# A four-layer transformer kernel on Trainium2: another order at the start of layer 0, at its seam with layer 1 and in layer 2, gates and experts' lists with the roles of their operands swapped, and experts every third slot

## The chip, the cores and the metric

The kernel runs on one core of one Trainium2 chip. TensorE (PE) multiplies matrices: it loads one operand, which stays (the stationary one, `lhsT`), and streams the other (the moving one, `rhs`) past it; results land in PSUM. VectorE (DVE), ScalarE (ACT) and GpSimd (POOL) do the rest, and SyncE (SP) issues most transfers. Every engine works through its own queue strictly in the order in which the kernel was written, and waits for others through semaphores. The metric is the device time of one execution in microseconds; lower is better.

## The reference

Four layers follow each other. Each is `x = x + attention(xn) + ffn(xn)` with `xn = layernorm(x)` over rows of 128; there are 4096 tokens in all.

- Layer 0, attention: an importance per token, relu(xn wi1) wi2, picks 76 tokens of each sequence of 256; 16 heads of 8 attend from all tokens to those. FFN: softmax gates over 8 experts; **each expert takes the 512 tokens with its highest gates** (of all 4096), computes `w2(silu(w1 x) * w3 x)`, and its rows are added back to their tokens.
- Layer 1, attention: 16 heads of 64 under a sparse causal mask. FFN: a sigmoid gate for each of 8 experts, the best two of each token, `down(relu(up(x w))**2)`.
- Layer 2, attention: 4 heads of 32 with learned windows. FFN: gated, then two hidden layers of 512 with gelu, then back to 128.
- Layer 3, attention: 16 heads of 64, causal. FFN: one quantized matrix and a low-rank one.

```python
x = x + L0_attn(xn) + L0_ffn(xn); xn = layernorm(x)
x = x + L1_attn(xn) + L1_ffn(xn); xn = layernorm(x)
x = x + L2_attn(xn) + L2_ffn(xn); xn = layernorm(x)
x = x + L3_attn(xn) + L3_ffn(xn)
```

All values are 32-bit floats, but for some masks and lists of integers in bf16, which holds them exactly.

## The kernel before, in words

**Tiling.** Tokens go in 8 chunks `c` of 512 (two sequences of 256; four tiles of 128 tokens with the token on the partition). `xnT` is a chunk turned, with the feature on the partition. PSUM has two double banks `sc`, two banks `tp`, one `mm` and one `po`. The order on all engines is written out by hand; no scheduler moves anything.

**Layer 0.** `begin` loads and normalizes chunks 0 to 3 and does the first chunk's preparation (`prelude`). Then `run` goes through slots `kk` from -8 to 69, eight to a chunk. In each slot it issues, for the chunk `c = kk // 8`, one `exps` (four scores of 32 rows and an exp over 1024 columns), for the next chunk one `maxima` (four more scores and their maxima on VectorE), and now and then `outputs`, `divided`, `turned` and `project`, which ends in `r[c]`, the chunk's attention. Beside them lanes advance by one step a slot. A lane is a generator; one step reaches to its next `yield`:

- `prelude(c + 2)`: importance (`ph`, `pi`), its column (`pcol`), ranks on VectorE, picks on GpSimd, queries (`queries0`), picked rows (`px`), keys (`pk`, then `ka` on GpSimd). `maxima` needs `ka`.
- `choice()`, from slot -3: 15 rounds find each expert's threshold bit by bit. A round compares on VectorE (`ge`), counts on TensorE and reduces on VectorE. Then come prefix sums and `vals`, the numbers of tokens as bf16.
- `expert(e)`, from slot `19 + 4 * e`: 0-1 comparisons with the places (`ohs`, four of 128 x 1024); the list `pix`, 32 matmuls that sum numbers under comparisons; ids; four gathers on GpSimd (`xr`); two slots on, the product with the gate on VectorE; transposes; up (four matmuls of 512 columns); down; and, nine slots after the start, four additions into `acc_d` in HBM by GpSimd's transfers.

`stats` and `root` are the two parts of a norm on VectorE, `apply` scales and shifts (three quarters on ScalarE, one on GpSimd), `turn` transposes and copies on ScalarE, `logits(c)` makes four matmuls with the turned chunk stationary and the 8 columns of `wg` moving, `gates` makes the softmax. `warm(n)` issues `n` matmuls of ones into an unused part of `po`; nothing reads their result. I call these fills. There are 122 of them. They sit in `begin` (62), at 6 a slot in slots -8, -7, -6 and -3 to 3.

**The seam.** When the experts have added their rows, `fetch(c)` reads a chunk of `acc_d` back on SP's queue (from slot 59 on; it waits for the last expert's additions) and `finish(c)` adds it to `r[c]` on GpSimd. Layer 1's norms, `Route.norms`, are lanes that start at slots 62 to 69; what is left of them goes on in layer 1's first steps. For each chunk they make stats, root, apply (all on ScalarE), transposes, and gates with the turned chunk stationary and 8 columns moving, followed by an exp.

**Layer 1** is a pipeline over 128 pairs of heads; `u` counts its steps from -5. A pair is projected, scored (first at `u = -3`), divided, turned and multiplied with its values. `Route.places`, the choice of two experts per token, goes beside it, one step a `u`, and must be done when `scatter` starts at `u = 14`.

**Layer 2** runs an iteration per chunk `f` with the attention of the next chunk `a` interleaved. `weights(f, 3)` transposes the last exps and copies them on VectorE (`p_eT`), `values(f, 1)` multiplies them (L1644), `back(f, 1)` turns and divides. They are issued like this:

```python
do(self.gated, f, 0); do(self.weights, f, 3)
do(self.gated, f, 1); do(self.values, f, 1); do(self.project, a, 0)
do(self.gated, f, 2); do(self.back, f, 1);   do(self.project, a, 1)
do(self.gated, f, 3);                        do(self.project, a, 2)
```

**Lines of the profile.** L354 fills; L406 turns of layer 0; L417 its logits; L456 and L461 a round's comparison and count; L546 and L558 an expert's comparisons and its list; L570 gathers; L577 product with the gate; L592 and L602 up and down; L616 additions to HBM; L736 maxima; L770 exps; L786 outputs; L1203, L1209, L1213, L1217 and L1221 the norms and gates at the seam (apply, transposes, copy, gates, exp). In rows of TensorE a 32-bit matmul counts as two (`x8` is four matmuls), a bf16 one as one.

## Time and profile before

| | |
|---|---|
| median of 3 runs | 2096.87 us (2095.76 to 2101.85) |
| the profiled execution | 2104.49 us, its span 2102.8 us |
| mean granted TensorE clock | 0.969 |
| TensorE busy | 2040.5 us, 97% |
| VectorE, ScalarE, GpSimd busy | 1217.0, 1081.9, 926.9 us |
| fills (L354) | 122, between 1.1 and 88.3 us |
| first maxima of slot -8 | 30.01 us |
| slot 0, slot 63 | 69.84, 377.21 us |
| layer 1's first scores | 425.5 us |
| layer 2, layer 3 from | 1086, about 1534 us |

The profile is of one execution. Busy time of TensorE is the time in which a matmul was under way, whatever its clock; the granted clock, given beside it as a share of full speed, says how fast it ran. In a list of rows in order of time, a bracket at a row's end tells how long the engine stood idle before it and who released it.

### The profile page before, as it was taken

How to read it: one execution, taken by the hardware profiler on the slowest of the kernel's cores; microseconds unless marked ns; L12 is line 12 of the kernel's file. 1: busy time of each engine (PE TensorE's matmuls, PEld its weight loads, DVE VectorE, ACT ScalarE, POOL GpSimd, SP SyncE). 2: the span in 40 equal slices, each digit the busy share in tenths (PEclk: the TensorE clock that was granted, in tenths of full speed). 3: DMA queues.
4: the chain of work that ended last, by engine and by line, in shares of the span. 5: the costliest groups of instructions: out<-in, count | busy, mean ns of one | idle time of the engine just before them, and what ended most of it. 6: DMA issues, size and time to landing. Idle time of an engine off the chain costs nothing.

```text
span 2102.8 us, 39083 instructions
## 1 busy us (share of the span) xinstructions
PE 2040.5 (97%) x13660; PEld 1392.1 (66%) x13660; DVE 1217.0 (58%) x4836; ACT 1081.9 (51%) x3166; POOL 926.9 (44%) x1360
## 2 busy tenths in 40 slices
PE   9999999799999999999999999999999999999998
PEld 6666666567777777776664555555477777777776
DVE  6777663586555544467774444443366566656654
ACT  3234454466665555565543444333376656566563
POOL 4005554336886555467661222233143444344433
PEclk7899999699999999999999999999999999999999
DMA  7500111400003444300010000000000000000000
GB/s 229 133 1 14 25 27 19 110 1 19 31 32 101 119 119 119 88 20 28 26 54 1 1 1 1 0 1 1 1 1 6 2 6 6 2 6 6 7 1 11
DMA packets 83208, 72.27 MB, mean 34 GB/s; under 512 B 14466, under 2 KB 74020, under 8 KB 82852
## 3 DMA queue, kind: packets, MB, share of 16 engines
q1 hardware_dynamic: 66352, 37.88, 6.3%
q0 software_dynamic: 15488, 31.61, 5.7%
q8 instruction: 108, 1.77, 0.3%
q14 instruction: 88, 0.72, 0.1%
q10 hardware_dynamic: 1172, 0.30, 0.1%
HBM read 49.70 MB, written 24.25 MB: 35 GB/s over the span
## 4 chain that ended last, share of the span: by engine, by line
PE 84%; DVE 9%; ACT 4%; issue 2%; POOL 1%; DMA 0%; DVEq 0%; POOLq 0%; ACTq 0%; SPq 0%
PE sc L1025 11%; PE sc L1688 10%; PE sc L1053 9%; PE po L1105 9%; PE tp L1091 8%; PE mm L1123 6%; PE sc L1038 5%; PE sc L770 2%; PE mm L1368 2%; PE tp L786 2%; PE sc L736 1%; ACT e L1070 1%; PE mm L1726 1%; PE sc L1601 1%; DVE e L1066 1%
## 5 line engine op out<-in xcount | busy, mean ns | idle before, releaser
L1081 POOL TENSOR_TENSOR e<-e,rs 128x256 f32<-128x256 f32 (+2 forms) x512 | 392.7, 788 | 528.2 <-DVE rs L1079 421.1
L1070 ACT ACTIVATE e<-e,mn 128x128 f32<-128x128 f32 (+2 forms) x1024 | 442.8, 434 | 124.6 <-DVE mn L1066 110.6
L1066 DVE CUSTOM_DVE_ANT_0 e<-sc,causal 128x128 f32<-128x128 f32 (+1 forms) x512 | 152.5, 354 | 175.3 <-PE sc L1053 175.3
L1092 DVE COPY eT<-tp 128x384 f32<-128x384 f32 x512 | 253.7, 537 | 0.1
L1066 DVE CUSTOM_DVE_ANT_0 e<-sc,sparse 128x128 f32<-128x128 f32 (+1 forms) x512 | 139.5, 328 | 162.7 <-PE sc L1053 147.2
L1688 PE MATMUL sc<-ff,h 128*128 128x512 f32 x512 | 229.8, 595 | 0.9 <-ACT ff L1703 0.5
L1091 PE MATMUL tp<-ident,e 128*128 128x128 f32 x1536 | 223.6, 282 | 0.0
L1091 PEld LDWEIGHTS tp<-ident,e 128*128 128x128 f32 x1536 | 163.6, 141 | 74.2 <-issue 54.0
L1070 ACT ACTIVATION_READ_ACCUMULATOR e<-e,mn 128x1 f32 x1024 | 191.4, 187 | 0.0
L1688 PEld LDWEIGHTS sc<-ff,h 128*128 128x128 f32 x512 | 93.4, 190 | 105.9 <-issue 101.2
L1123 PE MATMUL mm<-out,oT 128*128 128x128 f32 x1024 | 131.7, 283 | 7.8 <-ACT hb L1374 4.2
L1667 POOL TENSOR_TENSOR x<-l_o,x 128x256 f32<-128x256 f32 x16 | 11.9, 743 | 276.8 <-DVE l_o L1661 276.3
L1123 PEld LDWEIGHTS mm<-out,oT 128*128 128x128 f32 x1024 | 123.0, 197 | 14.9 <-ACT hb L1374 6.4
L1025 PE MATMUL sc<-m,qkv 128*128 128x256 f32 x512 | 126.1, 389 | 1.1 <-ACT m L1043 0.5
L1030 ACT ACTIVATE n<-sc 128x1024 f32<-128x1024 f32 x64 | 65.5, 1024 | 108.9 <-PE sc L1025 108.9
L1053 PE MATMUL sc<-n 64*128 64x128 f32 (+1 forms) x1024 | 118.5, 350 | 0.0
L1567 POOL TENSOR_SCALAR n<-dist,reach 128x256 f32<-128x256 f32 (+1 forms) x112 | 104.0, 929 | 18.8 <-DVE l_mn L1615 8.7
L1105 PE MATMUL po<-eT,p_v 128*64 128x256 f32 (+1 forms) x1024 | 111.5, 339 | 0.1
L1105 PE MATMUL po<-eT,m 128*64 128x256 f32 (+1 forms) x1024 | 111.4, 338 | 0.1
L1053 PE MATMUL sc<-qk 64*128 64x128 f32 (+1 forms) x1024 | 108.8, 331 | 1.4 <-DVE mn L1066 1.4
L1025 PEld LDWEIGHTS sc<-m,qkv 128*128 128x128 f32 x512 | 92.2, 190 | 20.3 <-ACT e L1070 7.9
L1030 ACT ACTIVATE qk<-sc 128x1024 f32<-128x1024 f32 x64 | 65.4, 1022 | 76.5 <-PE sc L1025 63.6
(399 smaller groups left out, 3827.5 us busy)
## 6 DMA issues: line engine op xcount, KB each, us to landing
xb<-zero SPq DMA_DIRECT2D x1, 4608.0 KB
xb<-xb SPq DMA_DIRECT2D x36, 128.0 KB
yb<-yb SPq DMA_DIRECT2D x36, 128.0 KB
x<-in_L_attn_x SPq DMA_DIRECT2D x8, 256.0 KB
m<-in_L_ffn_w SPq DMA_DIRECT2D x8, 256.0 KB
xn_d<-x SPq DMA_DIRECT2D x8, 256.0 KB
xa<-acc_d SPq DMA_DIRECT2D x8, 256.0 KB
h<-in_L_ffn_h_wT SPq DMA_DIRECT2D x2, 1024.0 KB
```

Source lines behind the costliest of these rows:

```text
L1025: nc.tensor.matmul(p[:, n, i * S : (i + 1) * S], lhsT=self.wqk[n][:, (2 * gg + i) * P : (2 * gg + i + 1) * P], rhs=(self.xk if n else self ...
L1030: self.pending.append(lambda: nc.scalar.activation(t.rearrange("p n i s -> p n (i s)"), p, AF.Copy))
L1038: nc.tensor.matmul(p[:, 0, t * S : (t + 1) * S], lhsT=self.xk[c][:, t0 : t0 + P], rhs=self.wv[:, gg * 256 : (gg + 1) * 256], start=True, s ...
L1053: nc.tensor.matmul(ps[:, j, c0:c1], lhsT=qk[r, 0, i, qt * P : (qt + 1) * P], rhs=qk[r, 1, i, k0 : k0 + c1 - c0], start=True, stop=True,)
L1066: nc.vector.tensor_tensor_reduce(out=e[:, j, c0:c1], in0=ps[:, j, c0:c1], in1=self.mask[:, c0:c1], scale=1.0, scalar=3e38, op0=ALU.add, op ...
L1070: nc.scalar.activation(e[:, j, c0:c1], e[:, j, c0:c1], AF.Exp, bias=m1, scale=-1.0, accum_out=sums[:, 2 * qt + j : 2 * qt + j + 1],)
L1081: nc.gpsimd.tensor_tensor(e[:, :, c0:c1], e[:, :, c0:c1], bcast(rs[:, 2 * qt : 2 * qt + 2], 2, c1 - c0), ALU.mult)
L1091: nc.tensor.transpose(pt[:, n * P : (n + 1) * P], e[:, j, c0 : c0 + P], k.ident)
L1092: nc.vector.tensor_copy(eT[:, j, :], pt[:, :384])
L1105: nc.tensor.matmul(o[64 * j : 64 * j + 64, t * P :], lhsT=v[:, t ^ self.swap, h : h + 64], rhs=eT[:, j, t * S : t * P + S], start=(t == 0) ...
L1123: nc.tensor.matmul(p[:, :D], lhsT=self.oT[s][:, n, t * P : (t + 1) * P], rhs=wo[:, n, :], start=(first is None and n == 0), stop=(n == 7),)
L1688: self.nc.tensor.matmul(ph, lhsT=self.w[wh][:, c, m * P : (m + 1) * P], rhs=src[c], start=(c == 0), stop=(c == NF - 1))
```

## The change

It has seven parts.

1. **Beginning.** Loads of `wg`, `wv` and `bv` go from ScalarE's queue to SP's. The norm of chunk 1 is by itself, and those of chunks 2 to 7 are one group of six; each apply, turn and logits step is dealt out to slots -8 to -4 with fills between. GpSimd's constants are made in three parts (`consts1` to `consts3`), two of them at slots -5 and -4. `prelude` issues the first query a slot earlier and `px` and `pk` on separate slots.
2. **Logits and layer 1's gates.** The gate matrix, padded to 32 columns, is stationary and four chunks' `xnT` of 512 columns each move, in four column groups of the array side by side. Four transposes bring the result back to tokens on partitions.
3. **Experts' lists.** The 8 columns of numbers are stationary and 128 columns of comparisons move; fourths of the tokens go to four column groups, after one matmul that zeroes the bank. ScalarE copies the four partial sums, and a slot later one matmul with `eighths` adds them up and turns them. The gathers stay in the same slot as before.
4. **Experts start every third slot**, at `19 + 3 * e`.
5. **The seam.** `fetch` goes out at slots 51 and 52 into tiles of its own, `finish` from slot 54. Layer 1's norms of chunks 0 to 6 are steps at fixed slots from 55 to 65 (`Route.early`, a quarter of the apply on GpSimd), gates of chunks 0 to 3 at 62 and 63. Chunk 7 and the other gates (`Route.last`) go before `places` in layer 1's first five steps.
6. **Fills**: 354 in all. 94 in `begin`; 5 a slot in -8 to 3, 2 in 12 to 18, 3 in 53 to 63, 5 from 64 on; 12 before the count of the choice's first two rounds and 4 before the others; 27 in the dealt-out steps; 4 in each of layer 1's first five steps.
7. **Layer 2.** `values(f, 1)` and `back(f, 1)` each move behind the next gated step.

```diff
 def logits(self, first):
-        for i in range(TT * c, TT * c + TT):
-            matmul(self.pg[:, i * NE : (i + 1) * NE], lhsT=self.xnT[c][:, i % TT * P : (i % TT + 1) * P], rhs=self.wg)
+        pl = self.bank()
+        for g in range(4):
+            nc.tensor.matmul(
+                pl[32 * g : 32 * g + 32, :], lhsT=self.wg, rhs=self.xnT[first + g], start=True, stop=True,
+                tile_position=(0, 32 * g),
+            )
+        rows = self.p2.tile([P, 2, CAP], F32, tag="g", name="lg", bufs=1)[:, 0, :]
+        nc.scalar.activation(rows, pl, AF.Copy)
+        yield
+        pt = self.bank()
+        for t in range(TT):
+            nc.tensor.transpose(pt[:, t * P : (t + 1) * P], rows[:, t * P : (t + 1) * P], k.ident)
+        nc.vector.tensor_copy(...)
 def choice(self):
+            self.warm(12 if i < 2 else 4)
 def expert(self, e):
         pix = k.po()
+        nc.tensor.matmul(pix[:, :P], lhsT=k.zero.bitcast(BF16)[:, :P], rhs=k.ones_b, start=True, stop=False)
         for t in range(32):
+            g = t % 4
             nc.tensor.matmul(
-                pix[:, :8], lhsT=ohs[t // 8][:, t % 8, :], rhs=self.vals[:, e, t, :, :].rearrange("p q v -> p (q v)"),
-                start=(t == 0), stop=(t == 31),
-            )
-        ixv = pix[:, :8].rearrange("p (q v) -> p q v", v=2)
+                pix[32 * g : 32 * g + 8, :P], lhsT=self.vals[:, e, t, :, :].rearrange("p q v -> p (q v)"),
+                rhs=ohs[t // 8][:, t % 8, :], start=False, stop=(t >= 28), tile_position=(0, 32 * g),
+            )
+        fourths = p2.tile([P, P], F32, tag="ohq", name="fourths")
+        nc.scalar.activation(fourths, pix[:, :P], AF.Copy)
+        yield
+        nc.tensor.matmul(pix[:, P : P + 8], lhsT=fourths, rhs=self.eighths, start=True, stop=True)
+        ixv = pix[:, P : P + 8].rearrange("p (q v) -> p q v", v=2)
...
         nc.vector.scalar_tensor_tensor(ids, ixv[:, :, 0], 128.0, two, ALU.mult, ALU.add)
-        yield
 def begin(self):
...
+            -8: [(self.stats, 6, 2, 6), (self.stats, 7, 2, 6), (self.root, 2, 6), (self.apply, 2), (self.apply, 3), warm],
+            -7: [
+                (self.turn, 2), warm, (self.apply, 4), (self.turn, 3), warm, (self.apply, 5), (next, a), warm,
+            ],
+            -6: [(self.turn, 4), (self.apply, 6), warm, (self.turn, 5), (next, a, 0), warm, (self.apply, 7), warm],
+            -5: [(self.turn, 6), warm, (self.turn, 7), warm, (next, b), (self.consts2,)],
+            -4: [(next, b, 0), (self.consts3,), (list, self.gates())],
 def run(self, tail):
-            starts[19 + 4 * e] = [self.expert(e)]
-        warm = {-8: 6, -7: 6, -6: 6, -3: 6, -2: 6, -1: 6, 0: 6, 1: 6, 2: 6, 3: 6}
-        loads = 19 + 4 * NE + 8
+            starts[19 + 3 * e] = [self.expert(e)]
+        warm = {kk: 5 for kk in range(-8, 4)} | {kk: 2 for kk in range(12, 19)} | {kk: 3 for kk in range(53, 64)}
+        loads = 19 + 3 * NE + 8
...
-                if kk == max(loads + c, 8 * c + 12) + 1:
-                    self.finish(c, xas.pop(c))
-                if kk == max(loads + c, 8 * c + 12):
-                    xas[c] = self.fetch(c)
+                if kk == loads + c // 4:
+                    xas[c] = self.fetch(c)
+                if kk == max(loads + 3 + c, 8 * c + 13):
+                    self.finish(c, xas.pop(c))
+            tail(kk)
+            if kk >= 64:
+                self.warm(5)
 class Route:
+    def early(self):
+        at = {}
+        for first, n in ((0, 2), (2, 2), (4, 2), (6, 1)):
+            for c in range(first, first + n):
+                u = 55 + c + c // 6
+                at.setdefault(u, []).append((self.stat, c, first, n))
+                for late, step in ((0, self.apply), (1, self.turn)):
+                    at.setdefault(57 + c + late, []).append((step, c))
+        at[62].append((self.gates, 0))
+        at[63].append((self.others, 0))
...
+    def last(self):
+        c = NC - 1
+        self.stat(c, c, 1); yield
+        self.root(c, 1); self.apply(c); yield
+        self.turn(c); yield
+        self.gates(c - 3); yield
+        self.others(c - 3)
 def layer1(...):
-    first = route.places()
+    first = chain(route.last(), route.places())
     def extra(u):
+        if u < 0:
+            warm(4)
 class Layer2:
             do(self.gated, f, 1)
-            if n:
-                do(self.values, f, 1)
             do(self.project, a, 0)
             do(self.gated, f, 2)
             if n:
-                do(self.back, f, 1)
+                do(self.values, f, 1)
             do(self.project, a, 1)
             do(self.gated, f, 3)
+            if n:
+                do(self.back, f, 1)
             do(self.project, a, 2)
```

`stat`, `root`, `apply`, `turn`, `gates` and `others` of `Route` do for layer 1 what `stats`, `root`, `apply`, `turn` and the two halves of `logits` do for layer 0; its `gates` puts the exp on the copy.

## The prediction

> **What bounds the kernel now.** I read the page's busy shares and slices first, then the busy time by stage, then TensorE's rows in order of time, then its waits.

> ```profile
> PE 2040.5 (97%) x13660; PEld 1392.1 (66%) x13660; DVE 1217.0 (58%) x4836; ACT 1081.9 (51%) x3166; POOL 926.9 (44%) x1360
> ...
> PEclk7899999699999999999999999999999999999999
> ```

> TensorE is busy nearly always, but its clock dips in the first slices and in the eighth. Stages (busy us, then clock, DMA share, GB/s):

> ```profile
> 0.00:30.00 30.00, 26.23 (x128) 17.58 (x128) 21.49 (x105) 10.75 (x20) 18.74 (x99) 0.83 0.87 264
> 30.00:59.80 29.80, 29.58 (x148) 23.05 (x148) 14.44 (x57) 9.26 (x20) 4.96 (x8) 0.61 0.51 139
> 69.84:166.30 96.46, 91.10 (x669) 57.46 (x668) 75.21 (x231) 32.20 (x43) 12.95 (x21) 0.89 0.19 55
> 166.30:318.84 152.54, 149.43 (x1270) 100.23 (x1269) 101.97 (x219) 75.19 (x98) 81.01 (x88) 0.99 0.15 23
> 318.84:377.21 58.37, 56.92 (x439) 36.62 (x439) 20.03 (x40) 28.78 (x38) 26.37 (x27) 0.91 0.20 28
> 377.21:425.50 48.29, 33.55 (x161) 26.29 (x160) 27.24 (x129) 22.84 (x58) 12.20 (x23) 0.61 0.38 107
> 1086.00:1534.00 448.00, 439.88 (x1900) 234.64 (x1898) 188.83 (x673) 183.50 (x452) 121.56 (x136) 0.99 0.01 2
> ```

> I chose the cuts by slots of layer 0: slot -8 (first maxima) starts at 30.01, slot 0 at 69.84, slot 20 at 166.30, slot 48 at 318.84, slot 63 at 377.21; layer 1's first scores are at 425.5. The join, 48.3 us, has the worst clock and 14.7 us of idle; the row above it is nearly pure TensorE work.

> ```profile
> 44.78 6.83 PE L417 MATMUL po<-wg,n 128*128 128x8 f32 x32
> ...
> 82.04 0.50 PE L461 MATMUL tp<-ge,ones_b 128*128 128x192 bf16 x4 [1.50 <-DVE ge L456]
> ...
> 84.01 3.22 PE L786 MATMUL tp<-a_p,vs 76*64 76x256 f32 x16
> ...
> 96.99 1.95 PE L786 MATMUL mm<-a_p,vs 76*64 76x256 f32 x16
> ...
> 305.45 0.95 PE L558 MATMUL po<-vals,m 128*128 128x8 bf16 x32
> ...
> 386.65 1.63 PE L1209 MATMUL mm<-ident,m 128*128 128x128 f32 x4 [4.23 <-ACT m L1203]
> ...
> 1253.59 0.86 PE L1644 MATMUL po<-p_eT,m 128*32 128x256 f32 x16
> ```

> The same 16 passes of outputs take 3.22 us in one place and 1.95 in another: half clock. In the join norms and gates alternate between TensorE and ScalarE, each waiting for the other.

> ```profile
> PE po L1644 <- DVE p_eT L1632: 3.8, 7, 1.2
> ```

> That is the only repeated wait in layer 2 (us, times, longest).

> **How I add.** I counted TensorE's instructions per slot in both orders and priced each at its full-clock start-to-start time from the rows: four exps 0.92, four maxima 0.61, eight outputs 1.88, one 512-wide query 0.86, an expert's up 3.6 and down 1.88, its list 0.87, one fill 0.125 (six from 30.73 to 31.48). To layer 1's scores: before 318.3 plus 122 fills = 15.2, in all 333.5; actual 425.5, so 92 us are lost to half clock and idle. After: 309.5 plus fills. Undisturbed slots take 1.05 times the sum (24 to 31: 42.6 against 44.9; 40 to 47: 41.6 against 43.7), so I use 1.05.

> **Fills: 122 become 354**: begin 62 to 94, slots -8 to -1 36 to 91, slots 0 to 19 24 to 86, slots 53 to 63 none to 33, 64 to 69 none to 30, layer 1's first five none to 20. 232 more at 0.125 are 29 us; where TensorE has no gap they are paid in full.

> **Begin, to slot 0: -11.5.** Chunk 0's transposed copy starts at 10.18 though its transposes end at 9.20: ScalarE was issuing loads, three of which move to SP's queue (there they delay only later loads and stores). That is 1.0. The importance column is copied at 17.48 though ScalarE finished it at 15.70, because VectorE was in the root of chunks 1 to 3; that becomes the root of chunk 1 alone, finished by then: with the 1.0, nearly 3. Full clock instead of 0.5 between 16 and 22: about 1.5. First maxima 25.5 instead of 30.0. The next stage becomes bound by ScalarE: stats and root of six chunks end near 33 on VectorE; then six applies of 3 x 0.41, six copies of 0.60, two logits copies of 0.60 and two queries of 0.69 end near 47. Gates take about 4. GpSimd's constants, now behind its applies, take 7 (vs 3.6, the rest 3.3) and end near 52; the choice needs the last, bits, so they may be the later of the two. Three slots with fills (5.3 + 4.9, overlapping that) put slot 0 near 58.5 instead of 69.84. The logits themselves fall from eight times 0.94 to two times 1.5 (four 512-wide at once 0.9, four transposes 0.5); L1644's row carries this: 1536 columns in 0.78 us, where one after the other they would be 2.58, so four column groups run 3.3 wide.

> **Slots 0 to 19: -0.5.** 62 more fills cost 7.8, with the factor 8.1; work is 0.9 more. Against it stand 10.6 us of missing clock (0.11 of 96.5) and 5.4 of idle. [...] The trace shows 1.50 us of idle before 82.04, then, cut every 4 us, a clock of 0.57 from 84 to 88 and 0.58 to 92. [...] I take the row: 7 of clock, 2.5 of idle. Fills do nothing where VectorE sets the pace (75.2 of 96.5 busy).

> **Slots 20 to 62: +6.** Experts every third slot move the same work forward; the sum over 20 to 62 goes from 193.3 to 202.1, with 3.8 of fills and the norms' transposes inside, so 212 with the factor, 2 more because slots 57 to 63 need 3.2 us of ScalarE each (exps 1.02, apply 1.25, copy 0.60, others 0.3), and 3 for clock drops (5.2 lost in 318 to 377 before). Against 210.9 that is +6. The list: 32 matmuls took 0.87, 27 ns each. By L1644's overlap the turned ones would need 22 ns (L461's 192 columns take 108 ns, 128 of them 72, by 3.3). [...] So 0.70 by the row, 0.80 by the rule; I keep L558's 27 ns, 0.87, and add zeroing 0.06 and the sum of fourths 0.24: +0.3 by eight, 2.4, in the sum above. Without overlap 72 ns, +14 over all. The copy of the fourths, about 0.25, lies on a ScalarE half idle. On GpSimd adds of one expert (228.76 to 236.3, 7.5 us) and gathers of the next but one (216.48 to 221.3, 5.0) now fall in one slot: 12.5 of some 20 us. The multiply two slots on may find its rows 1 to 2 us late; VectorE stalls, but the transposes come a slot later still. SP's fetches now go out at slots 51 and 52 into other buffers; the last adds should land near 52 and the first sum run at 54.

> **Join: -31.** Norms of chunks 0 to 6 are done by slot 65. From slot 63: 3 us of that slot, 9 for outputs, divide, turn, project with their copies (slots 64 to 69, fills in the gaps), 5 for layer 1's first projection, copy and scores (420.45 to 425.5 before): 17 instead of 48.3. **Entry of layer 1: +1**: chunk 7's norm, gates and turn in its first five slots, and the choice of experts starts a slot or two later, still before the scatter. **Layer 2: -3.5**: one projection and one gated pair, 2.6 us, pass before the values; the 3.8 us wait goes. Next late would be the way back, but its distance is kept.

> Sum -39.5. The profiled execution took 2104.49 (1.7 outside its span), 7.6 above the median; 2104.5 - 39.5 = 2065, less that 7.6 gives **2057.5**.

> **Rivals.** (1) *Slower by the fills.* If the 92 us lost stay lost, since gaps are VectorE's and ScalarE's and the clock does not follow fills, work falls by 8.8, fills add 29, layer 2 gives 3.5: +17, 2114. It decides from where fewer than 17 of the 92 come back. [...] Against it: the join alone has 31 us that fills did not make. 7%.
> (2) *GpSimd's bursts hold the experts.* Rows late by 4 us rather than 1.5, ka behind a burst near slot 38: 3 us by eight, 2081. For: 12.5 us bursts. Against: 81 of 152 busy. 12%.
> (3) *The join moves forward rather than away*: first sums wait for the adds, VectorE's stats stand behind them and slots 55 to 63 stretch by 1.7 each: +15, 2072. 15%.
> (4) *Lists do not overlap*, so the swap does not do what it says: +12, 2069. 10%.
> (5) *Clock full throughout*: 5 more in slots 0 to 19, 5 in 20 to 62: 2047. 12%.
> My forecast, 2048 to 2068: 40%; the rest, 4%, lies near no change.

> About 0.3%, 6.3 us, is what a measurement here can tell. Faster 0.89, same 0.04, slower 0.07. The range 2038 to 2084 leaves out (1), no change, and the far ends.

> **Right or wrong.** Right: slot 0 near 58, clock 0.9 or more from 30 on, first scores near 387, no p_eT wait in layer 2. Wrong: PE idle before experts' transposes (2), idle before the norms' transposes in slots 57 to 63 (3), list groups over 1.5 us (4), or slots 0 to 19 longer than 100 us with the clock still at 0.9 (1).

## The result, and the profile after

The changed kernel takes 2066.61 us (median of 4 runs, 2061.39 to 2069.17), the kernel before 2097.78 (median of 4, 2095.76 to 2101.85): a ratio of 0.9846 with a 95% interval of 0.9821 to 0.9870, 31 us less. The profiled execution took 2069.17 us, its span 2067.1. TensorE's row and its clock from the page:

```profile
PE 2016.7 (98%) x13836; PEld 1374.9 (67%) x13836; DVE 1212.2 (59%) x4841; ACT 1080.8 (52%) x3162; POOL 946.2 (46%) x1372
...
PEclk9996999999999999999999999999999999999999
```

The dips of the first slices and of the join are gone; a new one stands in the fourth slice. Busy time by stage, cut at slot -8, slot 0, slot 20, slot 48, slot 63, layer 1's first scores, and in layer 2 (busy us of PE, PEld, DVE, ACT and POOL, then clock, DMA share, GB/s). Slot 0 is cut here, as the other slots are, at its exps. In the kernel before they start at 70.84; the 69.84 given ahead is the matmul with `wi` just before them.

```profile
0.00:25.35 25.35, 22.63 (x144) 15.59 (x144) 18.72 (x98) 7.25 (x12) 11.23 (x42) 1.00 0.86 261
25.35:62.80 37.45, 33.04 (x244) 22.05 (x244) 24.33 (x89) 13.71 (x30) 14.36 (x71) 0.91 0.70 179
62.80:153.21 90.41, 87.75 (x732) 59.22 (x731) 72.97 (x225) 32.66 (x44) 10.51 (x18) 1.00 0.22 64
153.21:336.97 183.76, 173.48 (x1364) 112.67 (x1363) 109.61 (x229) 84.21 (x115) 111.54 (x108) 0.91 0.15 23
336.97:386.72 49.75, 49.26 (x425) 32.74 (x424) 29.49 (x121) 29.77 (x49) 21.21 (x21) 1.00 0.24 52
386.72:404.47 17.75, 15.31 (x122) 11.02 (x118) 6.35 (x30) 8.33 (x19) 4.10 (x11) 1.00 0.03 7
1065.00:1498.00 433.00, 429.82 (x1898) 232.61 (x1898) 188.82 (x674) 184.13 (x455) 122.81 (x137) 1.00 0.01 2
```

Slots 0 to 19 run at full clock, in 90.4 us instead of 95.5. The join is 17.75 us instead of 48.3. But slots 20 to 47 have a clock of 0.91 where they had 0.99, and slots 20 to 62 take 233.5 us instead of 210.9. TensorE's rows at the places that the prediction spoke of:

```profile
36.99 1.92 PE L436 MATMUL mm<-n,wg 128*32 128x512 f32 x8
...
163.71 0.62 PE L591 MATMUL po<-m,vals 128*8 128x128 bf16 x32 [1.94 <-POOL vals L565]
...
188.21 3.68 PE L825 MATMUL tp<-a_p,vs 76*64 76x256 f32 x16
...
205.07 1.95 PE L825 MATMUL tp<-a_p,vs 76*64 76x256 f32 x16
...
392.53 1.21 PE L1265 MATMUL tp<-ident,m 128*128 128x128 f32 x4 [0.63 <-ACT m L1259]
...
407.62 1.45 PE L1265 MATMUL tp<-ident,m 128*128 128x128 f32 x4 [1.77 <-ACT m L1259]
...
1290.36 0.86 PE L1738 MATMUL po<-p_eT,m 128*32 128x256 f32 x16
```

Four chunks' logits now take 1.92 us at half clock. The same sixteen passes of outputs take 3.68 us at 188 and 1.95 at 205: the half clock has moved to the experts. TensorE stands 1.94 us before the first list, for GpSimd's `vals`. In the join the longest wait for the norm's apply is 0.63 us, where it was 4.23. Where the time went, by stage, from the two profiles:

| | before | after | measured | predicted |
|---|---|---|---|---|
| start to slot 0 | 70.84 | 62.80 | -8.0 | -11.5 |
| slots 0 to 19 | 95.46 | 90.41 | -5.1 | -0.5 |
| slots 20 to 62 | 210.9 | 233.5 | +22.6 | +6 |
| join | 48.3 | 17.75 | -30.5 | -31 |
| first to fifth scores of layer 1 | 12.9 | 17.9 | +5.0 | +1 |
| rest of layer 1 | 670.7 | 665.1 | -5.6 | 0 |
| layers 2 and 3 | | | -14.0 | -3.5 |
| sum | | | -35.6 | -39.5 |

The sum is larger than the 31 us between medians because the profiled run of before lay 6.7 us above the median of its 4 runs, that of after 2.6. Cut every 4 us, the stage with the loss looks like this:

```profile
160.00:164.00 4.00, 2.06 (x40) 1.18 (x39) 3.83 (x5) 0.38 (x1) 3.66 (x2) 1.00 0.00 0
164.00:168.00 4.00, 4.00 (x45) 3.10 (x34) 0.86 (x2) 1.30 (x2) 0.00 (x0) 0.57 0.01 4
...
188.00:192.00 4.00, 4.00 (x22) 1.90 (x19) 0.86 (x2) 0.46 (x2) 0.00 (x0) 0.50 0.00 0
...
196.00:200.00 4.00, 4.00 (x18) 2.91 (x15) 3.97 (x9) 1.17 (x2) 3.53 (x4) 0.67 0.05 14
200.00:204.00 4.00, 4.00 (x15) 1.46 (x13) 2.78 (x11) 2.72 (x4) 3.22 (x5) 1.00 0.21 56
```

TensorE is idle for half of 160 to 164, and then runs at half clock, busy all the time, for 34 us. That costs 17 us. The kernel before had 13.8 us of half clock in these slots, so the clock makes 10 of the 22.6; the other 12 are the fills, the work moved ahead and its waits.

Two sums help to read all the runs below. The span times (1 - mean granted clock) is the clock lost in a run; the span times the clock is what the run would be without. Before: 2038 to 2041 and 52 to 61 lost (means over 45 runs beside three groups of kernels). The changed kernel: 2042.7 and 21.2 (4 runs). So the gain is clock; the rest cancels, above all layer 2's 14 us less against what the added fills cost (some 12 us, as a run below shows). Kernels of different groups ran beside their own runs of before (medians 2094.57, 2101.83 and 2095.16), so between groups a difference of 0.3% means little.

### The profile page after: what moved, and what is told of

The parts are those of the page before. It is cut to its first block, busy times and chain, and to the rows that moved or that the text cites. A ratio compares the mean times of both kernels' runs of the same rounds, so it can differ in the third digit from the quotient of the medians.

```text
span 2067.1 us, 39426 instructions
## 1 busy us (share of the span) xinstructions
PE 2016.7 (98%) x13836; PEld 1374.9 (67%) x13836; DVE 1212.2 (59%) x4841; ACT 1080.8 (52%) x3162; POOL 946.2 (46%) x1372
## 4 chain that ended last, share of the span: by engine, by line
PE 88%; DVE 6%; ACT 3%; POOL 1%; issue 1%; DMA 0%; SPq 0%; POOLq 0%; DVEq 0%; ACTq 0%
PE sc L1071 11%; PE sc L1782 11%; PE sc L1099 10%; PE po L1151 9%; PE tp L1137 9%; PE mm L1169 6%; PE sc L1084 6%; PE sc L809 3%; PE tp L825 2%; PE mm L1464 2%; PE sc L775 1%; PE mm L1820 1%; DVE e L1112 1%; PE sc L1774 1%; PE po L373 1%
## 5 line engine op out<-in xcount | busy, mean ns | idle before, releaser
L1661 POOL TENSOR_SCALAR n<-dist,reach 128x256 f32<-128x256 f32 (+1 forms) x112 | 104.3, 931 | 18.8 <-DVE l_mn L1709 8.7
L1071 PEld LDWEIGHTS sc<-m,qkv 128*128 128x128 f32 x512 | 92.2, 190 | 20.3 <-ACT e L1116 7.9
```

Source lines behind the costliest of these rows:

```text
L1071: nc.tensor.matmul(p[:, n, i * S : (i + 1) * S], lhsT=self.wqk[n][:, (2 * gg + i) * P : (2 * gg + i + 1) * P], rhs=(self.xk if n else self ...
```

## The experiments

My theory A: the wait for `vals` in slot 21 lowers the clock, and the small tiles after it cannot raise it. Rival B: turned lists and small tiles hold the clock down by themselves. For layer 2: the torn values group costs 14 us, against 3.5 by the sum of its idle rows. For fills: the row of before, in which the clock fell to 0.57 after 1.50 us of idle, against the first rival, that the clock does not follow fills.

**Fills before the first list.**

```diff
+        if e == 0:
+            self.warm(16)
         pix = k.po()
```

> The changed kernel with 16 fills (2.0 us at full clock) directly before the first expert's list at slot 21, where TensorE stood 1.94 us for GpSimd's vals and the clock then read 0.50 from 168 to 196. Theory A (that idle gap drops the clock, and the small tiles of slots 22 to 26 cannot raise it again until the first up matmuls): clock 0.95 or more from 164 to 200, slot 27 at about 186 instead of 202.9, the total about 16 us shorter, near 2050. Theory B (the turned lists, 8 columns wide in column groups, or the small tiles themselves keep the clock low; the gap is incidental): clock still near 0.5 in 168 to 196, and the total unchanged to +2.

Measured: 2067.29 us (2064.65 to 2073.18), ratio 0.9873 (0.9847 to 0.9900); sums 2044.4 and 21.7. Its stage by 4 us:

```profile
160.00:164.00 4.00, 3.94 (x63) 2.69 (x61) 3.37 (x5) 0.40 (x2) 3.21 (x2) 1.00 0.00 0
164.00:168.00 4.00, 4.00 (x42) 3.37 (x42) 2.47 (x9) 1.29 (x3) 0.27 (x1) 1.00 0.01 4
...
180.00:184.00 4.00, 3.21 (x16) 2.58 (x18) 3.69 (x14) 1.10 (x3) 0.00 (x0) 0.53 0.00 0
```

A holds for the place: with the gap filled the clock stays full from 160 to 180, over the same turned lists and tiles. But at 180.79 the first expert's transposes, now reached sooner, come after 1.88 us of waiting for the rows, and the clock is low for 6.8 us from 180.2 on; another 10.2 us stand at 262, after short idle stretches that the trace puts down to nothing (some records may be missing there). Slot 63 comes 4.8 us earlier in the profile, not 16, and the median shows no gain. One gap was cured and the next took its place.

**The list in its old roles**, all else as changed.

```diff
-                pix[32 * g : 32 * g + 8, :P], lhsT=self.vals[...], rhs=ohs[t // 8][:, t % 8, :],
-                start=False, stop=(t >= 28), tile_position=(0, 32 * g),
+                pix[:, :8], lhsT=ohs[t // 8][:, t % 8, :], rhs=self.vals[...],
+                start=(t == 0), stop=(t == 31),
```

> The changed kernel with the experts' lists as before: comparisons stationary, 8 columns of numbers moving, no zeroing, no sum of fourths; the slots stay. Theory A (the gap at slot 21): TensorE still waits about 2 us for vals, and the clock is still near 0.5 for some 30 us after; the total within 3 us of the changed kernel. Theory B (the turned lists hold the clock down): clock 0.95 or more from 164 to 200, the total about 16 us shorter. A list takes 0.87 us instead of 0.92 in either.

Measured: 2074.59 us (2068.24 to 2080.15), ratio 0.9908 (0.9881 to 0.9934); sums 2042.6 and 29.5. The wait is there (2.09 us) and the clock falls at the same place, so the turned list is not the cause. But the phase after it lasts 6.8 us, not 34; three others follow (180.8, 255.9, 266.1). Without clock the two kernels are alike, 2042.6 against 2042.7. But with old lists 29.5 us of clock are lost instead of 21.2, and the ratio's interval lies above the changed kernel's, so the turned lists seem to be worth up to 8 us, through the clock. The phase at 180.8 hints at how. It follows a step in which TensorE is busy throughout, with a list in its old roles in it:

```profile
177.40:180.81 3.41, 3.41 (x57) 2.57 (x58) 0.75 (x2) 0.72 (x2) 2.20 (x3) 1.00 0.18 46
180.81:184.22 3.41, 3.41 (x20) 2.07 (x16) 1.97 (x5) 1.37 (x2) 0.00 (x0) 0.50 0.08 20
```

```profile
177.62 0.96 PE L589 MATMUL po<-vals,m 128*128 128x8 bf16 x32
```

The kernel before has one such fall too (238.1, list at 235.6). Behind slot 0, none of the 26 falls read every 1 us in six profiles of kernels with turned lists follows a step without idle: the least is 0.55 us, before 382.2 with layer 1's gates in their old roles. Rival B is wrong about the turned list, and may be right about the old one; two falls do not show it.

**The changed kernel once more.**

> The changed kernel as it is, beside the other kernels of this group, so that all are told against it on one chip; and a second profile of it. If low-clock phases depend on where the clock's own steps of about 3.41 us fall against the gaps, the phase of 34 us after slot 21 need not come again: 3.4 to 10 us are as likely, and the phases stand elsewhere. If the stage itself makes it, it comes again at the same place with the same length. Total 2061 to 2069 as before.

Measured: 2069.03 us (2064.22 to 2074.18), ratio 0.9846 (0.9824 to 0.9869). I had expected another length; the phase of 34.1 us came again, right after the same wait (1.93 us, clock low from 166.5 to 200.6). What repeats is where the clock's steps fall against the wait: both times the wait ended 0.8 or 0.9 us before the fall. Other executions need not have it: those without a profile lost 14 to 35 us of clock.

**Fills behind the first list**, the gap left as it is.

```diff
         nc.scalar.activation(fourths, pix[:, :P], AF.Copy)
+        if e == 0:
+            self.pg = pix
+            self.warm(28)
         yield
```

> The changed kernel with 28 fills right behind the first expert's list at slot 21: the gap of 1.94 us before the list stays, so the clock falls as before. 28 fills are 3.5 us at full clock and 7 at half, at least one whole step of 3.41 us in which nothing but 128-row matmuls run. If a low phase ends only after a step filled mostly with tiles of 128 rows: the phase after slot 21 lasts 7 to 10 us instead of 34, and slot 63 comes 5 to 9 us earlier for all the fills. If any busy step ends it, or its length is set elsewhere: it still lasts 30 us or more, and slot 63 comes 7 us later.

Its rows and clock (the profiled run is 6.6 us later from its start on):

```profile
170.28 0.62 PE L591 MATMUL po<-m,vals 128*8 128x128 bf16 x32 [1.93 <-POOL vals L565]
171.33 4.82 PE L373 MATMUL po<-ones_b 128*128 128x256 bf16 x28 [0.43 <-ACT fourths L596]
```

```profile
168.00:172.00 4.00, 1.64 (x39) 1.11 (x38) 2.40 (x4) 0.66 (x2) 2.22 (x2) 0.90 0.02 4
172.00:176.00 4.00, 4.00 (x26) 2.96 (x24) 0.00 (x0) 0.00 (x0) 0.00 (x0) 0.67 0.00 0
176.00:180.00 4.00, 4.00 (x40) 3.29 (x40) 2.20 (x8) 1.02 (x1) 0.01 (x1) 1.00 0.00 0
```

The clock falls at 171.2 and is back at 174.6, while only fills run: one step of 3.4 us instead of ten. That fits what the 34 us seem to have needed: not time, nor work of any kind, but work of full tiles. It is one profile, and the fills are not the only way to such a step. With layer 1's gates in their old roles (below) the code up to slot 59 is that of the changed kernel, and the same wait of 1.93 us is followed by only 6.8 us. There the steps fall 0.8 us earlier against the work, and the transposes and the product with `wka`, which in the changed kernel a boundary divides between two steps, lie whole in the second:

```profile
167.50 1.12 PE L839 MATMUL tp<-ident,ov 128*128 128x128 f32 x4
168.41 0.64 PE L757 MATMUL mm<-wv,xsT 128*76 128x128 f32 x2
168.84 1.22 PE L732 MATMUL tp<-xsT,wka 128*128 128x152 f32 x4
```

So with the same work, in another place against the steps, the phase lasted 6.8 us and not 34.1. The fills do not make the kernel faster (2074.08 us, ratio 0.9893, 0.9877 to 0.9909; sums 2047.8 and 25.4): the fills cost 4.8 us, and phases of 3.4, 6.8 and 10.2 us follow at 195, 205 and 277.

**Without the choice's fills**, 76 of them.

```diff
-            self.warm(12 if i < 2 else 4)
```

> The changed kernel without the 76 fills before the counts of the choice's rounds (9.5 us of TensorE at full clock). [...] By the row of before (1.50 us idle, then 0.57): the clock in slots 0 to 19 falls to about 0.9 and they get 0 to 5 us longer. [...]

Measured: 2075.90 us (2068.02 to 2077.55), ratio 0.9897 (0.9865 to 0.9930); sums 2037.1 and 35.2. Slots 0 to 19 take 91.0 us (63.82 to 154.85) at a clock of 0.96, against 90.4 at full clock with the fills: the row's side. What the fills cost there they bring back. The total, against the changed kernel in another group, says 5.6 less without clock and 14 more lost. By these sums the 76 fills bring back what they cost, and a few us more.

**Without 200 fills**, all that stand where the kernel before had none.

```diff
-            self.warm(12 if i < 2 else 4)
-        warm = (self.warm, 3)
+        warm = (self.warm, 0)
-        warm = {kk: 5 for kk in range(-8, 4)} | {kk: 2 for kk in range(12, 19)} | {kk: 3 for kk in range(53, 64)}
+        warm = {kk: 5 for kk in range(-8, 4)}
-            if kk >= 64:
-                self.warm(5)
-        if u < 0:
-            warm(4)
```

> The changed kernel without 200 of its 354 fills: none before the choice's counts, none in the dealt-out norm steps, none in slots 12 to 18 and 53 to 69, none in the first five steps of layer 1; those of begin and of slots -8 to 3 stay. They are 25 us of TensorE at full clock. The prediction's first rival (the clock does not follow fills) gives 15 to 25 us less, near 2045. The row of before (fills that shorten gaps hold the clock) gives 0 to 10 us more, near 2072, with more than 10 us more of lost clock before layer 1's first scores.

Measured: 2070.25 us (2069.45 to 2078.31), ratio 0.9864 (0.9841 to 0.9886), beside 2069.03 of the changed kernel in the same group. Its clock on the page:

```profile
PEclk8998999799999999999999999999999999999999
```

Sums 2028.7 and 41.0 against 2041.1 and 25.6: of 25 us of fills half lay in gaps and cost nothing, the other 12.4 cost their time, and they won back 15.4 of clock. So the 200 fills are worth 1 us by the medians and 3 by the sums, which five runs of each cannot tell from nothing. The changed kernel's gain lies in its other edits, and in what the 154 fills left here, all of them ahead of slot 4, may do; those were not tried.

**Experts every third slot and norms early, alone, in the kernel before.**

```diff
-            starts[19 + 4 * e] = [self.expert(e)]
-        loads = 19 + 4 * NE + 8
+            starts[19 + 3 * e] = [self.expert(e)]
+        loads = 19 + 3 * NE + 8
-        at = {62: [0, 1], 64: [2, 3], 66: [4, 5], 68: [6], 69: [7]}
+        at = {55: [0, 1], 57: [2, 3], 59: [4, 5], 62: [6], 69: [7]}
```

> The kernel before with two edits alone: experts every third slot, and the norms of layer 1 as the same lanes as before but started at slots 55, 57, 59, 62 and 69 instead of 62 to 69. No fills, no turned gates, no turned lists, old begin, old layer 2. If the join is long because norms start too late: from slot 63 to layer 1's first scores 18 to 25 us instead of 48, slot 63 some 5 to 8 later for the work moved ahead of it, the total 18 to 28 us less. If it is the fills or the turned gates that shorten it: the join stays above 35 us at a clock of 0.6 or so, the total within 8 us of before.

Measured: 2113.51 us (2112.77 to 2116.05), ratio 1.0065 (1.0048 to 1.0081): slower, which neither side had expected. Its clock by stretch, and two rows:

```profile
390.00:400.00 10.00, 8.79 (x44) 5.84 (x44) 4.01 (x21) 5.45 (x13) 0.00 (x0) 0.61 0.01 2
...
420.00:430.00 10.00, 4.78 (x21) 4.11 (x21) 3.31 (x13) 1.49 (x6) 3.14 (x10) 0.50 0.05 11
```

```profile
404.91 1.87 PE L1217 MATMUL mm<-gate,n 128*128 128x8 f32 x8 [0.53 <-ACT oT L818]
...
433.21 1.63 PE L1209 MATMUL mm<-ident,m 128*128 128x128 f32 x4 [7.43 <-ACT m L1203]
```

The clock falls at 371.7, after a wait of 1.59 us for the norm that ends at 370.9, and with the norms' waits spread over 15 slots more of the outputs and scores now run at half clock; each gate takes 1.87 us. Chunk 7's norm still has to be ready before layer 1's first scores, and they wait 7.43 us for it. Slot 63 now starts at 398.15 instead of 377.21 and the join is still 40.5 us (to 438.61). Starting the norms sooner does not shorten it by itself.

**Layer 1's gates in their old roles**, all else as changed.

```diff
-        at[62].append((self.gates, 0))
-        at[63].append((self.others, 0))
+        for c in range(7):
+            at.setdefault(59 + c, []).append((self.gate1, c))
```

> The changed kernel with layer 1's gates in the roles of before (a turned chunk stationary, 8 columns moving, eight times, each a slot after its turn); norms stay at slots 55 to 65, fills stay. Eight times 0.94 us against two times 1.5: by size 4.5 us more, spread over slots 59 to 69, the join still under 22 us. If the turned gates are what lets the join shrink (the kernel before with early norms alone kept a join of 39 us, at half clock, with gates of 1.88 us each): a low phase through slots 60 to 69, a join above 28 us, 10 us or more in all.

Measured: 2075.43 us (2074.06 to 2081.08), ratio 0.9907 (0.9891 to 0.9922). Slots 20 to 62 and the join:

```profile
153.13:393.91 240.78, 226.31 (x1812) 152.40 (x1811) 139.28 (x349) 114.29 (x167) 132.72 (x128) 0.93 0.18 28
393.91:412.83 18.92, 17.39 (x139) 13.24 (x138) 6.31 (x30) 8.44 (x22) 4.10 (x11) 1.00 0.04 7
```

The join is 18.92 us at full clock; with the slots before it, 8.4 us more than the changed kernel (259.7 against 251.3). Both profiles have 34.1 us of half clock in these slots, so the 8.4 are not clock: 4.5 is the gates' size as forecast, the rest was not traced. So the turned gates are worth some 6 to 8 us, and are not what the short join hangs on. Without seam fills it was 15.0 us (the kernel without 200 fills, 390.66 to 405.70), with old gates 18.9: neither alone carries it. What remains of the difference to the kernel with early norms alone is that each step stands in a slot of its own, that a quarter of the apply is GpSimd's, and that chunk 7 goes behind layer 1's first scores; these were not told apart.

**Layer 2's order, taken away and alone.** The two edits are the diff's layer 2 part, undone in the changed kernel, and made in the kernel before.

> The changed kernel with values(f, 1) and back(f, 1) of layer 2 where they were before; all else as changed. By the sum of idle before p_eT (3.8 us, the prediction's step): about 3.5 us longer than the changed kernel. By the difference of the two profiles (iterations of 54.64 against 52.77 us, a values group torn in two): 12 to 14 us longer, near 2080, with the p_eT wait back seven times.

> The kernel before with layer 2's new order alone: values(f, 1) and back(f, 1) each behind the next gated step. By the sum of idle before p_eT (3.8 us, the prediction's step): 3.5 us less than before. By the length of layer 2's iterations in the two profiles (54.64 and 52.77 us): 13 to 14 us less, ratio 0.993. If the order also changes how much clock is lost elsewhere, as the 26 us between the run with layer 2's old order and the changed kernel's ratio on its chip would have it: 20 us or more.

Measured: undone, 2090.18 us (2082.65 to 2099.75, 20 runs), ratio 0.9984 (0.9970 to 0.9999), sums 2056.9 and 32.3; from layer 2's first hidden block to its last step its profile is 13.8 us longer (420.6 against 406.8). Alone, 2082.11 us (2076.24 to 2083.97), ratio 0.9927 (0.9912 to 0.9942), sums 2026.8 and 52.0 beside 2041.2 and 52.5. Both give 14 us, without clock: 14.2 more, 14.4 less. (The first also lost 11 us more clock than the changed kernel; its profile does not show where.) Before, with the rows of one iteration:

```profile
1314.98 0.63 PE L1644 MATMUL po<-p_eT,m 128*32 128x256 f32 x4
1316.04 1.30 PE L1644 MATMUL po<-p_eT,m 128*32 128x256 f32 x12 [0.44 <-DVE p_eT L1632]
1317.27 1.13 PE L1576 MATMUL mm<-m,qkv 128*128 128x512 f32 x2
```

The waits of the changed kernel with the old order:

```profile
PE po L1738 <- DVE p_eT L1726: 3.9, 7, 1.2
```

The list of waits shows 0.44 us. From 1314.98 to 1317.27 it is 2.29, where a whole group takes 0.79 (1290.36 to 1291.15 in the changed kernel). The other half hides in rows that count as busy.

**Fills in three gaps, and in five.**

```diff
+        if e == 0:
+            self.warm(16)
-        pix = k.po()
+        self.pg = pix = k.po()
+        if e == 0:
+            self.warm(14)
         pt = self.bank()
         for q in range(4):
             nc.tensor.transpose(pt[:, q * P : (q + 1) * P], xr[:, q, 0:D], k.ident)
-            warm(4)
+            warm(16 if u == -3 else 4)
```

> The changed kernel with fills in three gaps: 16 before the first expert's list, 14 before its transposes at slot 24 (where TensorE stood 1.88 us for the rows in the run with fills before the list alone), and 16 instead of 4 before the turn of chunk 7 in layer 1's third step (1.77 us). 42 more fills, 5.3 us, of which the gaps hide most. If each gap of over 1.7 us ends in one or more low steps: no low phase in 160 to 200 and in 400 to 415, 5 to 10 us less than the changed kernel on the same chip, near 2058. If the low phases come from the small tiles and not from gaps: phases elsewhere in their place, total within 3 us.

Measured: 2059.25 us (2059.09 to 2069.62), ratio 0.9817 (0.9793 to 0.9840); the changed kernel in the same group 2069.03. Sums 2045.0 and 14.4: 4 of the 5.3 us of fills are paid, and 11 us of clock come back. It is the fastest kernel here, ahead of the changed kernel by 7 us by these sums and by 10 by the medians; the intervals of the two ratios still overlap. Its slots 20 to 62 and its join, then the entry of layer 1:

```profile
153.53:377.59 224.06, 213.36 (x1817) 140.29 (x1816) 138.76 (x350) 113.91 (x164) 133.22 (x128) 0.98 0.19 30
377.59:395.33 17.74, 15.30 (x121) 11.02 (x117) 6.33 (x30) 8.33 (x19) 4.08 (x11) 1.00 0.03 7
```

```profile
396.11 1.92 PE L373 MATMUL po<-ones_b 128*128 128x256 bf16 x16
398.48 1.21 PE L1269 MATMUL tp<-ident,m 128*128 128x128 f32 x4 [0.45 <-ACT m L1263]
```

The clock stays full at the entry, and the first five scores take 15.3 us instead of 17.9. But that is not shown to be the fills' doing: four kernels without them (old list, no choice's fills, old layer 2, fills behind the list) wait 1.75 or 1.76 us there and take 15.3 us too. In the last of them a step's boundary at 417.0 divides the wait (TensorE is idle for 1.76 of the 2 us from 416.0), and the clock stays at 1.00. In slots 20 to 62 the low phases shrink from 34.1 us to 6.8.

For five gaps, 24 fills go before the first turn at slot -7 and 14 behind the first expert's up matmuls.

> The kernel with fills in three gaps, with two gaps more: 24 fills before the first turn at slot -7 (3.48 us of waiting for ScalarE's apply, a phase of 6.8 us after it) and 14 behind the first expert's up matmuls (2.04 us of waiting for g before the next scores, a phase of 6.8 us after it). 38 more fills, 4.8 us, nearly all inside the gaps. Each phase costs about 3.4 us: 3 to 7 us less than with three gaps, a ratio to before near 0.979, and a clock of 0.995 or more. If gaps between are enough to make phases elsewhere: no gain or 2 us more.

Measured: 2067.64 us (2063.48 to 2069.76), ratio 0.9871 (0.9855 to 0.9886), sums 2050.1 and 15.0. No gain on three that shows, with the two in different groups: 38 more fills cost 5.1 by the sums (3 of it may be the groups, whose kernels of before differ by that much) and won no clock. One stage shows why:

```profile
25.67:62.75 37.08, 34.88 (x268) 23.30 (x268) 24.34 (x89) 13.68 (x30) 14.31 (x71) 1.00 0.72 185
```

The clock is full now, and the stage is still 37.1 us instead of 37.4. A slow TensorE cost nothing there, which agrees with the prediction's reading that ScalarE and GpSimd set the pace.

## Why the prediction was right, and where it was not

The measured 2066.6 lies 9 us above the forecast 2057.5 and inside its range, and the kernel is faster, as foreseen. But two terms were wrong by much, in opposite directions, and that the sum came out near is partly luck.

- **Join, -31: right** (-30.5). Of it 18.8 were half clock (37.5 us at 0.5) and 12.3 idle (14.7 became 2.4). That norms and gates no longer wait for each other agrees with the rows. Which edit does it is open: without its fills or its turned gates the join stays short, and earlier norms alone leave it at 40.5.
- **Begin to slot 0, -11.5: too much** (-8.0). First maxima came at 25.35 (25.5), GpSimd's constants at 52.7 (52), gates at 52.0. The step that failed is "Three slots with fills (5.3 + 4.9, overlapping that)": the first count stands in TensorE's queue at slot -3 and runs at 57.72, so most of slots -3 to -1 follows it. From 52.7 to 62.8 are 10.1 us, the 5.3 and the 4.9 in full.
- **Slots 0 to 19, -0.5: too little** (-5.1). The term was "7 of clock, 2.5 of idle" won back by fills that cost 8.1. All 10 us of lost clock came back. But the kernel without 200 fills needs 89.3 us here, so the gain is there without them. Before, TensorE waited twice 1.5 us or more for `ge`, and 20.3 us of low phases lie in this stage; in the kernel without 200 fills the longest wait for `ge` is 1.0 (a new one, for `qa`, is 1.9), and 7 us of low phases fall in the stage. The steps of the preparation dealt out over more slots are the only other edits there; they were not tried alone.
- **Slots 20 to 62, +6: the large miss** (+22.6). "3 for clock drops" was the term; 17 came from one phase of 34 us; the rest of the stage is 2 us over its 214. That `vals` is ready later than TensorE gets there was not in the working, and this is the step that failed: slot 20 came 13.1 us earlier, `vals` only 8.6 (ready at 172.3 before, 3.0 ahead of the list, and now at 163.7). So TensorE waited 1.94 us for it. The list's own step was right in size: 32 matmuls take 0.55 us (163.71 to 164.26), 17 ns each, less than L558's 27 ns, which the term kept, and than the row's 22. The 0.80 us "by the rule" beside them is shown by no run.
- **Entry of layer 1, +1: too little** (+5.0): chunk 7's turn waits 1.77 us, and two steps of half clock, which cost 3.4, lie on it. In four kernels without any edit to it, one of them with the wait divided at 417.0, the entry takes 15.3.
- **Layer 2, -3.5: the second large miss** (-14), shown twice. The mechanism was right; the term was taken from the list of waits, and should have been read from start to start: six times 2.29 and once 3.08 (1476.11 to 1479.19) against 0.79 is 11.3; the other 2.7 us were not traced.
- **Rest of layer 1**: 0 predicted, -5.6 in the two profiles, mostly low phases that only before's profile has (at 992 and 1033) or has longer (at 1085, 6.8 us against 3.4).
- **Rival 1** (fills come to nothing) was right on fills in the main: 200 of them are worth 1 to 3 us, within the noise. It was wrong that the 92 us lost would stay lost without them. The rivals of GpSimd's bursts, of the seam moving forward and of lists that don't overlap did not come.
- **Signs.** No p_eT wait is left in layer 2, as forecast. Slot 0 (62.8, not 58) and the first scores (404.5, not 387) missed, and the clock was 0.5 for 34 us in the midst of what was to be 0.9 or more. Of the four signs of being wrong none showed but for 0.7 us of idle before one expert's transposes.

## What to carry to other kernels

A stage that comes earlier meets inputs that have not moved: for each step pulled forward, list what its first instruction waits for, and when that is ready. Price a wait from the start of one group to the start of the next, not from the idle column. Count fills by the clock that they save at a named gap: 42 at three gaps came with some 7 us less here, 200 spread about with 1 to 3. And do not put the length of a low phase down to the code alone: the same code had 34 us of it twice and 6.8 once, where the steps fell otherwise.

## What the runs showed of the hardware

A gap inside a step was enough for a fall; one wait shows it. Layer 1 has a wait of 1.85 us for VectorE, between 960 and 1003. In four profiles (before, fills behind the first list, layer 1's gates in their old roles, fills in five gaps) it lies whole within a step, and the clock fell at the step's end (before: the wait from 989.43 to 991.28, the fall at 992.48). In two a boundary cuts it, the longer part 0.97 us (after) and 1.39 us (the kernel before with layer 2's new order), and the clock stayed. Another, of 1.78 us 40 to 42 us later in the same six, agrees. It lies whole within a step in three, with a fall in each: before at 1033.44, and with the fills behind the list and the old gates its row takes 3.50 and 3.46 us where it takes 2.05 at full clock. It is cut in three, the longer part 1.01 to 1.53 us, with no fall. The changed kernel, boundary at 973.5:

```profile
968.00:972.00 4.00, 4.00 (x29) 2.54 (x28) 2.61 (x13) 2.55 (x8) 2.64 (x5) 1.00 0.12 35
972.00:976.00 4.00, 2.15 (x15) 1.54 (x14) 2.41 (x7) 0.26 (x2) 2.94 (x4) 1.00 0.09 24
976.00:980.00 4.00, 4.00 (x34) 2.88 (x32) 2.08 (x12) 2.00 (x8) 0.52 (x1) 1.00 0.05 13
```

With layer 2's old order, the same wait, boundary at 975.3:

```profile
972.00:976.00 4.00, 2.15 (x14) 1.80 (x14) 2.15 (x6) 0.00 (x0) 2.66 (x4) 0.92 0.10 33
976.00:980.00 4.00, 4.00 (x22) 2.91 (x22) 0.73 (x6) 0.65 (x2) 0.00 (x0) 0.66 0.00 0
```

That may be why executions of one kernel lose different amounts of clock (14 to 29 us in the four of the changed kernel); it was not tested. Neither 1.5 nor 1.75 us of waiting told by itself whether the clock fell, and what ran in the rest of the step may count too. In the prediction's own row, the wait that ends at 82.04, only 0.92 us lay in the step whose end at 84.5 brought the fall; small tiles (32 x 76, 32 x 128, 76 x 64) filled most of the rest. In the kernel before with early norms 1.84 us of idle stood in one step (197.7 to 201.1) beside long matmuls, three of them in the microsecond from 198, and the clock stayed.

Nor was being busy enough to raise it. For before and after I weighted TensorE's busy time in each step by the size of its tile (rows times columns, as a share of 128 x 128, the largest tile in the rows). In layer 0's slots the clock stayed low after all 13 low steps with a weight of 0.58 or less, and rose after all 7 with 0.72 or more. In the 34 us phase nine steps of 0.19 to 0.54 went by at 100% busy (much of it tiles of 32 x 76, 32 x 128 and 76 x 64), and the tenth, 0.72, with transposes and a 512-wide query, ended it. The 28 fills behind the list (0.97 in their step) are a direct test of it, and with old gates the second low step, which weighs 0.70 by the three rows given above from 167.50 on alone, ended its phase. In these two profiles the weight went with the rise, not with the fall: before, a step of 0.22 at full clock was followed by another at full clock. At the start and at the seam of before the weighting does not hold (low steps of up to 1.00 were followed by low ones); many of the matmuls there move only 8 columns (L417, 32 rows at 44.78), but whether that is why was not tested.
